# A gated image scan on one core: the bank of the neighbour sum, the grouping of the projections, the joined bypass and the issue order

## Chip, cores and metric

The kernel runs on one NeuronCore of a Trainium2 chip. The metric is the device time of one execution in microseconds (us). Everything is fp32. "PE" is TensorE, "DVE" VectorE, "ACT" ScalarE, "POOL" GpSimd.

## What is computed

Two layers run one after the other on x of shape (8, 192, 64, 64). Only the first is touched by the change. Cut to what matters, its scan is:

```python
x = conv3x3_depthwise(conv1x1(x, W_in)) + b_dw          # 384 channels
p = conv1x1(x, W_xd)                                    # 16 channels
Gl, Gm, Gr = normalize_w(W_w @ p)                       # each divided by |Gl|+|Gm|+|Gr|+1e-7
xs = stack of 4 directions of x                         # x, x^T, and both flipped
def step(h, (x, l, gl, gm, gr)):                        # 8 steps along chunks of 8
    return l * x + gl * h_up + gm * h + gr * h_down
out = scan(step) * (W_u @ p) + xs * (W_d @ p)
y = sum over directions d of w_m[d] * out[d]            # then layernorm, GRN, conv1x1
```

The second layer (layernorm and two Mamba passes over the tokens) takes the larger part of the time; its code is the same on both sides.

## The kernel before

**Stages.** For each of the 8 images, `project` makes the depthwise convolution `xc` (three tiles of 128 channels) and the 16 proxy channels `xp`, `scan` runs the gated scan, `norm` and `project_out` finish. Only `scan` and the parts of `Step` that it calls are touched.

**Steps.** A scan has 96 steps: 3 channel tiles x 8 chunk positions j x 4 directions d, in this order, d innermost. One step works on 128 channels x 512 pixels. Its state is `h{d}`, so that step (j, d) needs the state of the step four before it. A step with j = 0 has no previous state: it has no gates, no neighbours, no normalization, and its state is simply lam times x.

**Parts of a step.** The six projections are matmuls of 16 rows (L237), each on its own 32-row group of the array by `ROWS`: GL group 0, GM 1, GR 2, GLAM 3 (`gates`), GU group 0 and GD group 1 (`up`). Then:

- `magnitude` (ACT, L250 for the first two, L247 in place for the third) takes absolute values; `norm` (DVE, L278, two adds) sums them in the third gate's bank; `log` and `exp` (ACT, L283, L288) and `newton` (DVE, L294, L295) make the reciprocal.
- `neighbour` (DVE, L263, three products of a gate with the shifted state); `pair` (POOL, L267) adds two of them; `total` (PE, L273, two identity matmuls) sums the rest in PSUM; `mix` (DVE, L299) multiplies by the reciprocal.
- `decay` (ACT, L254) copies the lam projection out of PSUM, `entry` (POOL, L257) multiplies it by x, `state` (POOL, L303) makes the new state.
- `direct` (ACT, L310) copies the D projection out of PSUM, `bypass` (POOL, L313) multiplies it by x; `output` (DVE, L319, `hu`) multiplies the U projection by the state.
- `add` (PE, L329, identity matmuls) sums `hu` and `dx` of the four directions in bank `yp`; `store` (ACT, L339, after every fourth step) copies it out.

**The joined bypass.** With `JOINED = 2`, direction 2 does not send its `dx` to PE; at direction 3 an extra POOL add (L315) puts the two `dx` together, and one matmul takes both.

**PSUM.** There are eight banks: `gl`, `gm`, `q`, `yp` one each, `gr` and `c` two each. `c` turns over three tiles in each step: the lam projection, the D projection and the U projection. The sum over neighbours has `q`.

**The order.** The steps are software-pipelined. One iteration of `scan` issues parts of five steps, named `s3` (oldest) to `s0` and `ahead` (next). The order of the lines in that loop is the order in each engine's queue; every engine works its own queue in order and waits where an operand or a buffer is not ready. In the loop PE gets, in order: total, gates, add, add, up.

Of the kernel before, what the change touches and what calls it, by code (L numbers as in the profile page):

```python
# [22 lines left out]
ND = 4  # L23
# [7 lines left out]
SLOTS = NC * GROUPS  # L31
FAR = (0, 5, 6, 10, 21, 23)
ACT_SET = "natural_log_exp_and_others"
JOINED = 2
GL, GM, GR, GLAM, GU, GD = range(6)

ROWS = {GL: (0, 0), GM: (1, 0), GR: (2, 0), GLAM: (3, 0), GU: (0, 1), GD: (1, 1)}
# [3 lines left out]
def kernel(ctx: ExitStack, tc: tile.TileContext, x, w_in, dw, vecs, w_xd, w_gate, w_m, w_out, mid):  # L41
# [4 lines left out]
    nc = tc.nc  # L46
# [10 lines left out]
    def bank(tag, name, shape=(P, T)):  # L57

        return ps.tile(list(shape), F32, tag=tag, name=name, bufs=2 if tag in ("gr", "c") else 1)


    ident = const.tile([P, P], F32, name="ident0")
# [139 lines left out]
    def direction(xc, d, j):  # L202

        if d % 2 == 0:
            at = j if d == 0 else CHUNK - 1 - j
            v = xc.rearrange("p h (n j) -> p j n h", j=CHUNK)[:, at]
        else:
            at = j if d == 1 else CHUNK - 1 - j
            v = xc.rearrange("p (n j) w -> p j n w", j=CHUNK)[:, at]
        return v if d < 2 else v[:, ::-1, :]  # L210

    def flat(ap):
        return ap.rearrange("p n h -> p (n h)")
# [4 lines left out]
    class Step:  # L218
# [19 lines left out]
            return dst  # L238

        def gates(self):  # L240
            self.pl = self.gate(GLAM, "c")
            if self.j:
                self.g = [self.gate(kind, tag) for kind, tag in ((GL, "gl"), (GM, "gm"), (GR, "gr"))]

# [23 lines left out]

        def total(self):
            if self.j:  # L270
                self.sum = bank("q", f"q_{self.tag}")
                for i, term in enumerate((self.q[2], self.q[0])):
                    nc.tensor.matmul(self.sum, ident, flat(term), start=(i == 0), stop=(i == 1))  # L273

# [36 lines left out]

        def bypass(self):
            nc.gpsimd.tensor_mul(self.dx, self.dx, direction(self.xc, self.d, self.j))  # L313
            if self.d == JOINED + 1:
                nc.gpsimd.tensor_add(self.dx, self.dx, self.before.dx)  # L315

        def output(self):
            self.hu = self.work("hu")
# [1 line left out]

        def add(self, i):


            if self.d == 0 and i == 0:
                self.yp = bank("yp", f"yp_{self.tag}")
            elif i == 0:
                self.yp = self.before.yp
            if i == 0 or self.d != JOINED:
                nc.tensor.matmul(  # L329
                    self.yp,  # L330
                    ident,
                    flat((self.hu, self.dx)[i]),
                    start=(self.d == 0 and i == 0),
                    stop=(self.d == ND - 1 and i == 1),
                )

        def store(self):
            if self.d == ND - 1:
# [8 lines left out]
    def scan(b, xc, xp):  # L347


        ys, steps = [], [Nothing()] * 4  # L350
        for c in range(NC):
            wg = w_gate_sb[:, :, :, c * P : (c + 1) * P]
            ys.append(big.tile([P, CHUNK, CHUNK * HW], F32, tag="big", name=f"y_{b}_{c}"))
            for j in range(CHUNK):
                steps += [Step(f"{b}_{c}_{j}_{d}", xc[c], xp, wg, d, j) for d in range(ND)]
                for step in steps[-ND:]:
                    step.y = ys[c][:, j, :]
        for before, step in zip(steps[4:], steps[5:]):
            step.before = before
        steps += [Nothing()] * 4  # L360
        for s3, s2, s1, s0, ahead in zip(steps, steps[1:], steps[2:], steps[3:], steps[4:]):
            s2.state()
            s0.neighbour(2)
            s0.neighbour(0)
            s0.entry()
            s1.newton()
            s1.total()
            s0.neighbour(1)
            s0.pair()
            s0.magnitude(2)  # L370
            s2.direct()
            ahead.gates()
            s0.norm()
            s0.log()
            ahead.decay()
            s2.bypass()
            s3.add(0)
            s2.output()
            s3.add(1)
            ahead.magnitude(0)  # L380
            s1.up()
            s0.exp()
            s1.mix()
            ahead.magnitude(1)
            s3.store()
        return ys

    def norm(b, ys):
# [112 lines left out]
    with tc.manual_schedule():  # L501
        leaving = iter(())
        for b in range(B):
            xc, xp = project(b, leaving)
            ys = scan(b, xc, xp)
            leaving = project_out(b, ys, norm(b, ys))
        for _ in leaving:
            pass
# [497 lines left out]
```

## Time and profile before

| | us |
|---|---|
| median of 3 runs (17370.91 to 17383.58) | 17378.43 |
| the profiled execution, its own time | 17372.38 |
| its span, first to last instruction | 17370.6 |
| the 8 scans together (first lam copy to last y copy of each) | 4463.8 |
| each scan | 551.4 to 565.5 |
| first layer, about | 6080 |

A page of the profile lists busy time by engine, the span in 40 slices, the chain of work that ended last, and groups of instructions with mean duration. The timeline lists instructions of one engine in order: start, duration, line, tiles, count, and in brackets the idle time before it with what ended it. An fp32 matmul shows as two records; "x4" is two matmuls. "PEclk" is the granted share of TensorE's full clock. Durations overlap a little where an engine is fed without a break: DVE products last 0.68 us but start 0.60 us apart.

### The profile page before, as it was taken

Reading aid. Unit: us, or ns where it says so; the run is one execution under the profiler, and the core shown is the slowest. Engines: PE = TensorE matmul, PEld = TensorE weight load, DVE = VectorE, ACT = ScalarE, POOL = GpSimd, SP = SyncE. Lnnn points to the kernel's source line nnn. Section 1 sums busy time; section 2 is a strip of 40 time slices with the busy share of each in tenths; the row PEclk is TensorE's granted clock in tenths of the full one; section 3 lists DMA queues with packets and bytes.
Section 4 is the critical chain, followed back from the end, with each engine's and each line's share of the span. In section 5 each row is a group of like instructions: output and inputs, shape, how many; then the busy total and the mean of one; then the engine's idle time right before and its main releaser. Section 6 shows DMA issues by size and latency. Waiting matters only on the chain.

```text
span 17370.6 us, 150062 instructions
## 1 busy us (share of the span) xinstructions
PE 16036.3 (92%) x42192; PEld 6487.9 (37%) x42192; DVE 15678.3 (90%) x17290; ACT 11433.8 (66%) x21275; POOL 15638.3 (90%) x9538
## 2 busy tenths in 40 slices
PE   8999999999999889999999999999999999999998
PEld 2333333333333334333334434344434343434433
DVE  8888878878888689999999999999999999999999
ACT  5656666566666566666666666666666666666666
POOL 7787967869787699999999999999999999999999
PEclk8999999999999999999999999999999999999999
DMA  0000000000000022222222222222222222222222
GB/s 13 10 6 15 1 15 4 11 15 1 15 1 13 13 102 102 102 102 102 103 101 103 102 103 101 97 99 96 100 101 102 102 102 102 103 102 103 102 103 81
DMA packets 392024, 1195.85 MB, mean 69 GB/s; under 512 B 43736, under 2 KB 110640, under 8 KB 389648
## 3 DMA queue, kind: packets, MB, share of 16 engines
q1 hardware_dynamic: 390784, 1185.97, 19.7%
q8 instruction: 330, 5.41, 0.1%
q14 instruction: 510, 4.18, 0.1%
q10 hardware_dynamic: 400, 0.29, 0.0%
HBM read 1127.39 MB, written 58.72 MB: 68 GB/s over the span
## 4 chain that ended last, share of the span: by engine, by line
POOL 23%; DVE 17%; PE 11%; ACT 11%; issue 8%; DMA 1%; POOLq 0%; DVEq 0%; SPq 0%; ACTq 0%
DVE da L799 12%; POOL hs L786 12%; ACT da L792 4%; POOL hs L813 4%; PE yp L818 3%; DVE hs L813 2%; PE pc L670 2%; DVE hs L799 2%; POOL lg L725 2%; POOL dt L727 2%; POOL e L723 2%; PE pi L648 1%; PE g L237 1%; ACT xc L683 1%; POOL dtx L730 1%
## 5 line engine op out<-in xcount | busy, mean ns | idle before, releaser
L786 POOL TENSOR_TENSOR hs<-dtx,b_sb 128x1024 f32<-128x1024 f32 x3072 | 7163.0, 2359 | 91.5 <-PE yp L818 69.9
L818 PE MATMUL yp<-hs,ident 128*128 128x512 f32 x12288 | 5814.5, 616 | 509.2 <-DVE hs L813 303.9
L799 DVE TENSOR_TENSOR_SCAN da<-da,state,hs 128x512 f32<-128x512 f32 x4032 | 5183.2, 1286 | 227.0 <-ACT state L809 140.3
L792 ACT ACTIVATE da<-dt,a 128x512 f32<-128x512 f32 x6144 | 4245.2, 691 | 195.2 <-POOL dt L727 4.1
L818 PEld LDWEIGHTS yp<-hs,ident 128*128 128x128 f32 x12288 | 2325.7, 196 | 3668.1 <-issue 2487.7
L813 DVE TENSOR_TENSOR hs<-da,c_sb 128x1024 f32<-128x1024 f32 x2304 | 2815.3, 1222 | 139.5 <-DVE da L799 2.7
L237 PE MATMUL g<-xp,w_gate_sb 16*128 16x512 f32 x8640 | 1815.6, 658 | 60.4 <-ACT dx L310 51.6
L809 ACT COPY state<-da 128x2 f32<-128x2 f32 x2304 | 358.1, 155 | 2293.8 <-DVE hs L813 2290.3
L813 POOL TENSOR_TENSOR hs<-hs,c_sb 128x1024 f32<-128x1024 f32 x768 | 1810.0, 2357 | 12.4 <-ACT state L809 12.4
L648 PE MATMUL pi<-xT,in_w 96*128 96x512 f32 x3072 | 1513.0, 630 | 264.6 <-ACT xc L674 174.9
L799 DVE TENSOR_TENSOR_SCAN hs<-da,state,hs 128x512 f32<-128x512 f32 x1344 | 1624.3, 1263 | 106.4 <-ACT state L809 106.4
L670 PE MATMUL pc<-xr,conv_diag 128*128 128x512 f32 x3072 | 1489.0, 615 | 5.3 <-POOL xr L659 3.0
L263 DVE TENSOR_TENSOR q<-g,h 128x512 f32<-128x512 f32 x2016 | 1352.0, 684 | 116.1 <-PE g L237 71.4
L273 PE MATMUL q<-q,ident 128*128 128x512 f32 x2688 | 1336.3, 620 | 0.0
L313 POOL TENSOR_TENSOR dx<-dx,xc 128x512 f32<-128x512 f32 x768 | 1080.1, 1406 | 158.6 <-ACT dx L310 136.9
L283 ACT ACTIVATE rc<-g,eps 128x512 f32<-128x512 f32 x672 | 462.4, 688 | 1115.0 <-DVE g L278 1115.0
L267 POOL TENSOR_TENSOR q<-q,q 128x512 f32<-128x512 f32 x672 | 853.7, 1270 | 197.4 <-DVE q L263 193.0
L648 PEld LDWEIGHTS pi<-xT,in_w 96*128 96x128 f32 x3072 | 597.1, 199 | 1104.0 <-issue 649.8
L237 PEld LDWEIGHTS g<-xp,w_gate_sb 16*128 16x128 f32 x8640 | 495.6, 188 | 1307.0 <-DVE q L263 392.0
L257 POOL TENSOR_TENSOR lam<-lam,xc 128x512 f32<-128x512 f32 x672 | 942.8, 1403 | 33.5 <-ACT lam L254 33.5
L163 POOL TENSOR_TENSOR xc<-xc,side 128x504 f32<-128x504 f32 x384 | 450.6, 1174 | 559.5 <-DVE xc L158 297.3
L278 DVE TENSOR_TENSOR g<-g,ab 128x512 f32<-128x512 f32 x1344 | 933.1, 694 | 22.8
(135 smaller groups left out, 23252.6 us busy)
## 6 DMA issues: line engine op xcount, KB each, us to landing
b_sb<-bc SPq DMA_DIRECT2D x1024, 512.0 KB, 7.2
c_sb<-bc SPq DMA_DIRECT2D x1024, 512.0 KB, 6.3
xin<-in_x_dram SPq DMA_DIRECT2D x64, 384.0 KB, 3.6
mid<-ot SPq DMA_DIRECT2D x16, 1536.0 KB, 8.4
xt<-mid SPq DMA_DIRECT2D x64, 384.0 KB, 5.0
out_dram<-y SPq DMA_DIRECT2D x64, 384.0 KB, 2.6
bc<-dbl SPq DMA_DIRECT2D x128, 64.0 KB, 1.6
in_w<-in_in_w_dram SPq DMA_DIRECT2D x2, 576.0 KB, 5.8
```

Of the source, the lines that this page charges most:

```text
L237: nc.tensor.matmul(dst, self.wg[r, at, self.d, :], flat(self.xp[r, self.j]), start=True, stop=True)
L257: nc.gpsimd.tensor_mul(self.lam if self.j else self.hc, self.lam, direction(self.xc, self.d, self.j))
L263: nc.vector.tensor_mul(self.q[i], rows(self.g[i]), self.h[:, :, i : i + HW])
L273: nc.tensor.matmul(self.sum, ident, flat(term), start=(i == 0), stop=(i == 1))
L313: nc.gpsimd.tensor_mul(self.dx, self.dx, direction(self.xc, self.d, self.j))
L648: nc.tensor.matmul(pi, self.m.in_w[:, i, c * P : (c + 1) * P], self.tokens.xT[:, i, :], start=(i == 0), stop=(i == 1))
L670: nc.tensor.matmul(pc, self.m.conv_w[:, c, t, :], self.xr[c][:, t : t + T], start=(t == 0), stop=(t == 3))
L786: nc.gpsimd.tensor_mul(self.hs, dtx, self.p.b_sb[self.g])
L792: nc.scalar.activation(self.da[:, n, :], self.p.dt[self.c], AF.Exp, scale=self.p.m.a[:, self.c, at : at + 1])
L799: nc.vector.tensor_tensor_scan(self.h[:, n, :], self.da[:, n, :], self.hs[:, n, :], 0.0 if self.p.k == 0 else self.state[:, n : n + 1], AL ...
L813: engine.tensor_mul(self.hs, self.h, self.p.c_sb[self.g])
L818: nc.tensor.matmul(self.p.yp[self.c], ident, self.hs[:, n, :], start=False, stop=stop)
```

## The change

Four things at once, all in the first layer's scan:

1. The lam projection goes to bank `q` (it was in `c`), and the sum over neighbours goes to `gl`, the bank that held the first gate (it was in `q`). So `total` has to wait until the first gate was read, and the next first gate until `mix` has read the sum.
2. `up` and `gates` stand next to each other, so that PE gets six 16-row projections in a row, and the adds and the total (four 128-row matmuls) in a row.
3. The joined bypass is gone: every direction sends its own `dx` to PE, and POOL has no extra add.
4. The whole order of the loop is another. `entry` is one iteration later, the first two `magnitude` parts one iteration later.

```diff
-JOINED = 2
...
         def gates(self):
-            self.pl = self.gate(GLAM, "c")
+            self.pl = self.gate(GLAM, "q")
...
         def total(self):
             if self.j:
-                self.sum = bank("q", f"q_{self.tag}")
+                self.sum = bank("gl", f"q_{self.tag}")
...
         def bypass(self):
             nc.gpsimd.tensor_mul(self.dx, self.dx, direction(self.xc, self.d, self.j))
-            if self.d == JOINED + 1:
-                nc.gpsimd.tensor_add(self.dx, self.dx, self.before.dx)
...
-            if i == 0 or self.d != JOINED:
-                nc.tensor.matmul(
+            nc.tensor.matmul(
...
         for s3, s2, s1, s0, ahead in zip(steps, steps[1:], steps[2:], steps[3:], steps[4:]):
+            s3.add(0)
+            s0.neighbour(0)
+            s3.add(1)
+            s0.magnitude(0)
+            s0.neighbour(2)
+            s2.direct()
             s2.state()
-            s0.neighbour(2)
-            s0.neighbour(0)
-            s0.entry()
+            s0.neighbour(1)
+            s2.bypass()
+            s1.total()
+            s0.magnitude(2)
             s1.newton()
-            s1.total()
-            s0.neighbour(1)
+            s2.output()
+            s1.mix()
+            s0.magnitude(1)
+            s1.up()
+            ahead.gates()
             s0.pair()
-            s0.magnitude(2)
-            s2.direct()
-            ahead.gates()
+            s3.store()
+            s1.entry()
             s0.norm()
+            ahead.decay()
             s0.log()
-            ahead.decay()
-            s2.bypass()
-            s3.add(0)
-            s2.output()
-            s3.add(1)
-            ahead.magnitude(0)
-            s1.up()
             s0.exp()
-            s1.mix()
-            ahead.magnitude(1)
-            s3.store()
         return ys
```

More of the change, by code (lines that the diff above doesn't have):

```diff
@@ L327, in add @@
                 self.yp = self.before.yp
-            if i == 0 or self.d != JOINED:
[L329 to L335, printed above, removed]
+            nc.tensor.matmul(
+                self.yp,
+                ident,
+                flat((self.hu, self.dx)[i]),
+                start=(self.d == 0 and i == 0),
+                stop=(self.d == ND - 1 and i == 1),
+            )
         def store(self):
```

## Prediction, made before the changed kernel was run

> **What bounds it now.** I read the page's slices first (the scans lie in the first 14 of 40, the rest is the second layer, which keeps its code), then the busy time by stretch inside one scan, then PE's timeline of one step, then DVE's and ACT's.
>
> ```profile
> 204.00:227.00 23.00, 23.00 (x80) 7.48 (x78) 22.58 (x37) 15.44 (x30) 22.06 (x18) 1.00 0.00 0
> 227.00:250.00 23.00, 23.00 (x80) 7.49 (x78) 22.57 (x37) 15.45 (x30) 21.84 (x17) 1.00 0.01 1
> 319.00:346.00 27.00, 24.13 (x54) 7.11 (x56) 7.63 (x12) 7.83 (x14) 16.38 (x13) 0.75 0.00 0
> ```
>
> Columns: stretch, its length, busy PE, PE weight loads, DVE, ACT, POOL, granted clock, DMA. The first two rows are four steps with j > 0 (the y copies stand 22.97 apart there): PE never stops, DVE and POOL are within 5% of full. Three engines are nearly tied, so relief on PE alone is worth at most the distance to the next. The third row is the passage from one channel tile to the next, where four steps have j = 0: DVE is idle for most of it and TensorE has only 0.75 of its clock.
>
> ```profile
> 307.22 1.98 PE L273 MATMUL q<-q,ident 128*128 128x512 f32 x4
> 309.13 1.14 PE L237 MATMUL g<-xp,w_gate_sb 16*128 16x512 f32 x8
> 310.20 1.12 PE L329 MATMUL yp<-hu,ident 128*128 128x512 f32 x2
> 311.17 1.02 PE L329 MATMUL yp<-dx,ident 128*128 128x512 f32 x2
> 312.12 1.13 PE L237 MATMUL g<-xp,w_gate_sb 16*128 16x512 f32 x4
> ```
>
> One step of PE: total 1.91, four gates side by side 1.07, two adds 1.92, up 1.06; the next total follows at 313.18. That is 5.96. The step without its second add (direction 2) took 5.10. 3 x 5.96 + 5.10 = 22.98, the measured 22.97. A lone matmul costs 1.06 and a second one of the same form only 0.86 more, so every change between 128-row and 16-row form costs 0.20, four times per step.
>
> ```profile
> 308.90 1.42 DVE L278 TENSOR_TENSOR g<-g,ab 128x512 f32<-128x512 f32 x2
> 310.23 0.68 DVE L319 TENSOR_TENSOR hu<-g,h 128x512 f32<-128x512 f32 x1
> 310.83 0.68 DVE L299 TENSOR_TENSOR rc<-q,rc 128x512 f32<-128x512 f32 x1
> ...
> 310.36 0.69 ACT L283 ACTIVATE rc<-g,eps 128x512 f32<-128x512 f32 x1 [2.02 <-DVE g L278]
> 310.94 0.58 ACT L254 COPY lam<-g 128x512 f32<-128x512 f32 x1
> 311.41 0.61 ACT L250 ACTIVATE ab<-g 128x512 f32<-128x512 f32 x1
> 311.90 0.64 ACT L288 ACTIVATE rc<-rc 128x512 f32<-128x512 f32 x1
> 312.42 0.61 ACT L250 ACTIVATE ab<-g 128x512 f32<-128x512 f32 x1
> ```
>
> DVE's timeline stands above the dots, ACT's below. ACT waits 2.02 for the norm and then does other copies between log and exp; nothing of PE hangs on the end of this sequence today.
>
> **Engine sums after the change, j > 0.** PE: four 128-row matmuls 1.06 + 3 x 0.86 = 3.64; six projections in two rounds (GU and GL share group 0, GD and GM group 1) 1.06 + 0.86 = 1.92; together 5.56 in every step, against 5.74 on average now. The missing join costs PE 0.86 in one step of four, and that is in this sum. POOL loses the 1.27 us add (192 times, 244 us): from about 22 to about 21 in four steps; it is no longer near the limit. DVE keeps its nine operations: starts 0.60 apart, 0.72 where one reads the one before (newton, norm): 7 x 0.60 + 2 x 0.72 = 5.65. So by sums alone a step could fall from 5.74 to about 5.65.
>
> **The new waits, j > 0.** Sums don't set the step; two closed loops through the engines do.
>
> *Loop A* (the `gl` bank and ACT's order). `total` may not write `gl` before the first magnitude has read it; that magnitude now stands behind log and exp of the step before in ACT's queue; log waits for norm, norm stands behind mix on DVE, mix waits for total. Round it goes: magnitude 0.61, to PE 0.05 (matmuls start 0.05 after an ACT release elsewhere), total 1.98 to its last end, to DVE 0.04, mix to norm 0.60, norm 1.42, to ACT 0.04, log 0.69, exp 0.03 behind it, exp to magnitude 0.52 (311.90 to 312.42). Sum 5.98.
>
> *Loop B* (banks `c` and `gl`). First neighbour to hu on DVE 0.60 + 0.60 + 0.60 + 0.72 + 0.61 = 3.13, hu 0.68, to PE 0.05, GU 0.53 + 0.43, GL behind it in the same row group 0.43 + 0.59, to DVE 0.04. Sum 5.88.
>
> Loop A is longer than all sums: 5.98 per step, 23.9 for four, +0.93 against 22.97. Behind the waiting total stand up and gates, behind ACT's log stand exp and the first magnitude. Bounds: the first weight load of a group is exposed (1.06 against 0.86 includes about 0.1 of it); if it hides under the wait, A is 5.87 and B 5.78, that is +0.5 for four steps. If total's wait for two engines costs 0.1 more, as DVE's starts after two semaphores do here, 6.08, +1.35. I take 5.98, since every term is a row. A scan has 18 such intervals between y copies: 18 x 0.93 = +16.7 (+9 to +24).
>
> **The passages with j = 0.** Two in each scan. The two y intervals of a passage sum to 49.2 on average over all 16 (44.5 to 55.1). Here PE waits for ACT:
>
> ```profile
> 328.60 2.08 PE L237 MATMUL g<-xp,w_gate_sb 16*128 16x512 f32 x4
> 331.42 2.07 PE L237 MATMUL g<-xp,w_gate_sb 16*128 16x512 f32 x2 [0.74 <-ACT dx L310]
> 333.42 2.08 PE L329 MATMUL yp<-hu,ident 128*128 128x512 f32 x2
> 335.29 1.91 PE L329 MATMUL yp<-dx,ident 128*128 128x512 f32 x2
> ```
>
> lam, D and U turn over two `c` banks, so the next lam projection waits for the D copy of the step before; that spreads the matmuls, the clock is halved (2.08 where 1.13 stood), and this delays the copies again. After the change lam has its own bank, and between two passages of 16-row work lie only adds. PE's work for the eight steps: two normal 2 x 5.98, two with total but one row round 4.70, two with neither 2.97, two with six projections and no total 3.84: 34.9. Following the new order through with these durations leaves PE waiting about 2 us for hu (three times 0.3 to 0.9). I take 37.1 at full clock. Bounds: 34.9, and 44.6 if as much is lost beyond PE's work as today (the same count gives 39.5 of 49.2 now, 9.7 over). Gain per passage 12.1 (4.6 to 14.3), twice per scan: -24.2.
>
> **A rule against the row.** The Trainium skill, "TensorE: Matmul & The Clock Gate", Part 1, The HAM clock gate, says that the clock returns to half after at least one idle window of about 3.4 us. Between 319 and 346 the longest pause of PE is 0.74 us, and yet the clock is 0.75: a stretch thinly filled with 16-row matmuls is enough. By the rule the passage would hold no half clock to win back: PE ran at half for a half of 27 us, 6.7 us of it lost, so 42.5 and a gain of 5.4; the scan would come out at 16.7 - 10.8 - 0.7 = +5.2, or +42 us in all. By the row the gain is 12.1. I take the row.
>
> The ends of a scan (first lam copy, last flush of 14.3) change by under 1 us: -0.7, from GL's shorter way at the start and the later store. The stages around the scan keep their instructions; the second layer is as before.
>
> **Sum.** Per scan +16.7 - 24.2 - 0.7 = -8.2; eight scans -66. The profiled execution 17372 gives 17306; the median of the runs is 6 above that execution, so 17312.
>
> **Rivals.**
> 1. *The passages stay cold* (slower side). If the j = 0 stretch keeps today's losses, the gain is 4.6 each: 16.7 - 9.2 - 0.7 = +6.8 per scan, +54, 17432. It decides from a gain below 8 per passage. For it: the clock fell without a long pause. Against: the cause of the pauses, the shared `c` bank, goes. 17%.
> 2. *The loops are shorter* (weight loads hidden): +9 - 24.2 - 0.7 = -16 per scan, -127, 17251. For it: loads are hidden wherever the group is busy. 22%.
> 3. *Passages warm, but loop A at 6.08*: 24 - 24.2 - 0.7 = -1 per scan, 17371, no change. 14%.
> 4. *The six projections don't run as two rounds*, so that GL, GM and GR follow one by one: PE +0.86 or more per step, 6.4, above loop A; 18 x 2.6 = 47, +180 us. The four gates side by side in 1.07 speak against it. 3%.
> The forecast as it stands: 44%.
>
> Forecast and rival 2 lie below -0.2% (-35 us, what a measurement of this kernel can tell from no change), with a part of the first near it: faster 0.66, within 0.2% 0.18, slower 0.16. The range runs from rival 2 with the shorter passages (17230) to rival 1 (17430).
>
> **What would show it.** y copies 23.9 apart inside a channel tile (22.97 now); PE no longer at 100% there, with `total` waiting about 0.3 for ACT's magnitude; log, exp and magnitude in one unbroken row; passages of 37 with the clock at 1.00; no L315 on POOL. Wrong would be: passages above 41, y copies below 23.4 or above 24.4, or any change in the second layer beyond a few us.

## The result, and the profile after

The changed kernel takes 17363.65 us (median of 12 runs, 17340.23 to 17373.36) and the kernel before, run on the same chip, 17373.88 us (12 runs, 17366.26 to 17383.58). The ratio is 0.9992, with an interval of 0.9983 to 1.0000: no change by the bound of 0.2%. The forecast was 17312, a change of -66 us that did not come; its range, 17230 to 17430, held the time because it reached from well below to above the kernel before. The profiled execution took 17365.81 us, its span 17364.0 (before: 17370.6).

The intervals between y copies, taken from the trace, say where the scan's time went. "Passage" is the sum of the two y intervals of a j = 0 stretch, "head" the time from the first lam copy to the first y copy, "flush" the last y interval.

| per scan | forecast of the change | before | after | difference |
|---|---|---|---|---|
| 18 steady intervals | +16.7 | 22.98 | 24.19 | 18 x 1.21 = +21.7 |
| 2 passages | -24.2 | 49.15 (44.5 to 55.1) | 37.9 (37.3 to 39.0) | 2 x -11.25 = -22.5 |
| flush | -0.7 with the head | 14.29 | 17.69 | +3.4 |
| head | | 31.7 | 28.89 | -2.8 |
| sum | -8.2 | | | -0.2 |

So the gain in the passages is there, and the slower steps give it back. All eight scans together take 4462.4 us (4463.8 before): 1.4 less. The spans differ by 6.6 us, and 6.4 of that lie behind the last scan, in code that is the same on both sides, so nothing shows that the 10 us between the medians come from the scan. The head is no fixed time: in the changed kernel it takes 26.1 to 33.5 us, with 6.8 to 23.9 us of it at half clock by the trace's clock records, which list the stretches at each granted clock (31.6 to 31.8 and 13.7 before).

The busy time by stretch of the changed kernel (stretch, its length, PE, PE weight loads, DVE, ACT, POOL, granted clock, DMA): four steps with j > 0, then a passage.

```profile
204.00:228.00 24.00, 23.09 (x81) 7.94 (x80) 22.53 (x37) 15.77 (x29) 20.88 (x17) 1.00 0.00 1
318.00:344.00 26.00, 25.26 (x79) 8.66 (x80) 16.66 (x26) 14.12 (x26) 23.29 (x18) 1.00 0.01 1
```

In the first row no engine is full any more: PE 96%, DVE 94%, POOL 87%. A stretch that no engine fills and that still repeats exactly points to a chain of waits through several of them. In the second row the clock is 1.00 where it was 0.75. PE's timeline of one step of the changed kernel shows the wait:

```profile
254.08 1.98 PE L272 MATMUL q<-q,ident 128*128 128x512 f32 x4 [0.23 <-ACT ab L249]
255.99 1.99 PE L236 MATMUL g<-xp,w_gate_sb 16*128 16x512 f32 x12
257.91 1.13 PE L324 MATMUL yp<-hu,ident 128*128 128x512 f32 x2
258.87 1.02 PE L324 MATMUL yp<-dx,ident 128*128 128x512 f32 x2
260.12 1.98 PE L272 MATMUL q<-q,ident 128*128 128x512 f32 x4 [0.23 <-ACT ab L249]
```

The totals are 6.04 apart, and each waits 0.23 for a magnitude of ACT. ACT in the same step:

```profile
258.23 0.69 ACT L282 ACTIVATE rc<-g,eps 128x512 f32<-128x512 f32 x1 [0.36 <-DVE g L277]
258.95 0.63 ACT L287 ACTIVATE rc<-rc 128x512 f32<-128x512 f32 x1
259.49 0.58 ACT L249 ACTIVATE ab<-g 128x512 f32<-128x512 f32 x1
```

Log, exp and magnitude stand in one row, as loop A has it. DVE, where log's wait for the norm begins:

```profile
256.10 0.69 DVE L298 TENSOR_TENSOR rc<-q,rc 128x512 f32<-128x512 f32 x1 [0.23 <-PE q L272]
256.70 1.49 DVE L277 TENSOR_TENSOR g<-g,ab 128x512 f32<-128x512 f32 x2
258.11 1.88 DVE L262 TENSOR_TENSOR q<-g,h 128x512 f32<-128x512 f32 x3
259.90 0.69 DVE L293 SCALAR_TENSOR_TENSOR g<-g,rc 128x512 f32<-128x512 f32 x1
...
261.23 0.68 DVE L316 TENSOR_TENSOR hu<-g,h 128x512 f32<-128x512 f32 x1
```

Mix waits for total (0.23), the norm pair follows and log follows that. All links of loop A can be read off these three views.

### The profile page after: what moved, and what is told of

Same layout as the page of the kernel before. It is cut to its first block, busy times and chain, and to the rows that moved or that the text cites. A ratio compares the mean times of both kernels' runs of the same rounds, so it can differ in the third digit from the quotient of the medians.

```text
span 17364.0 us, 152244 instructions
## 1 busy us (share of the span) xinstructions
PE 15944.2 (92%) x42576; PEld 6558.0 (38%) x42576; DVE 15697.1 (90%) x17290; ACT 11507.9 (66%) x21275; POOL 15419.6 (89%) x9346
## 4 chain that ended last, share of the span: by engine, by line
POOL 22%; DVE 18%; ACT 11%; PE 9%; issue 8%; DMA 0%; POOLq 0%; DVEq 0%; SPq 0%; ACTq 0%
DVE da L794 12%; POOL hs L781 12%; ACT da L787 4%; POOL hs L808 4%; PE yp L813 3%; DVE hs L808 3%; PE pc L665 2%; DVE hs L794 2%; POOL lg L720 2%; POOL dt L722 2%; POOL e L718 1%; PE pi L643 1%; ACT xc L678 1%; POOL dtx L725 1%; ACT z L679 1%
## 5 line engine op out<-in xcount | busy, mean ns | idle before, releaser
L236 PE MATMUL g<-xp,w_gate_sb 16*128 16x512 f32 x8640 | 1544.4, 630 | 26.8 <-ACT lam L253 10.7
L262 DVE TENSOR_TENSOR q<-g,h 128x512 f32<-128x512 f32 x2016 | 1262.1, 681 | 98.6 <-PE g L236 96.2
L253 ACT COPY lam<-g 128x512 f32<-128x512 f32 x768 | 449.4, 585 | 1330.1 <-PE g L236 1269.2
L157 DVE SCALAR_TENSOR_TENSOR xc<-pi,dw_sb,xc 128x504 f32<-128x504 f32 (+3 forms) x1152 | 834.2, 736 | 105.2 <-ACT xc L135 58.5
L302 POOL TENSOR_TENSOR h<-lam,rc 128x512 f32<-128x512 f32 x672 | 859.0, 1278 | 54.5 <-DVE rc L298 1.9
```

What stands on the lines that cost most here:

```text
L236: nc.tensor.matmul(dst, self.wg[r, at, self.d, :], flat(self.xp[r, self.j]), start=True, stop=True)
L262: nc.vector.tensor_mul(self.q[i], rows(self.g[i]), self.h[:, :, i : i + HW])
```

## The experiments

The theory was loop A: total waits for the magnitude, which stands behind log and exp, which wait for norm, mix and the total before. The expectations call it A. Its rivals were the count of matmuls on PE, loop B (first neighbour, hu, adds and gates in the same row group), and, for the passages, the half clock against the order of work. Line numbers of an experiment can differ from those of the changed kernel by a few.

**1. The join put back into the changed kernel.**

```diff
+            if self.d == JOINED + 1:
+                nc.gpsimd.tensor_add(self.dx, self.dx, self.before.dx)
...
+            if i == 0 or self.d != JOINED:
                 nc.tensor.matmul(self.yp, ident, flat((self.hu, self.dx)[i]), ...)
```

> The changed kernel with the joined bypass restored: one add less on TensorE in every fourth step, one 1.27 us add more on GpSimd. Theory A (the closed loop total, mix, norm, log, exp, first magnitude, total sets the step; TensorE waits 0.23 us in it): the y copies stay 24.2 apart (24.1 to 24.4) and the time stays within 25 us of the changed kernel's 17364. Rival P (the number of matmuls sets the step, so that the dropped join is what made it slower): 0.86 less in four steps, 23.3, and about 124 us less in all, 17240.

Measured: 17433.4 us (5 runs, 17422.0 to 17444.9), ratio 1.0035 (1.0023 to 1.0047). In undisturbed stretches the y copies stay 24.18 apart although PE does one add less per four steps, so PE's count of matmuls does not set the step. But the time rose by 70 us, not within 25: the steady intervals average 24.34 because 13 of 144 are about 25.9, the passages are 40.77 and the flush 19.24. By the clock records each of these 13 holds one stretch of 3.41 us at half clock and no steady interval of the changed kernel holds any; all eight scans spend 268 us at half clock, 126 in the changed kernel. PE's timeline in a passage of this kernel, then at the same place of the changed kernel, shows how it comes about:

```profile
333.42 1.12 PE L328 MATMUL yp<-hu,ident 128*128 128x512 f32 x2
335.67 1.14 PE L237 MATMUL g<-xp,w_gate_sb 16*128 16x512 f32 x6 [1.13 <-DVE hu L319]
336.74 1.99 PE L328 MATMUL yp<-hu,ident 128*128 128x512 f32 x2
338.51 1.90 PE L328 MATMUL yp<-dx,ident 128*128 128x512 f32 x2
```

```profile
335.29 1.13 PE L324 MATMUL yp<-hu,ident 128*128 128x512 f32 x2
336.25 1.02 PE L324 MATMUL yp<-dx,ident 128*128 128x512 f32 x2
337.55 1.14 PE L236 MATMUL g<-xp,w_gate_sb 16*128 16x512 f32 x6 [0.28 <-DVE hu L316]
```

PE waits 1.13 for a hu where the changed kernel waits 0.28. The hu is not later: in front of it DVE waits 2.02 for POOL's state, 2.03 in the changed kernel. PE is earlier, by the add that direction 2 no longer sends. In the 3.42 us up to 336.86 PE is busy for 2.29 (in the changed kernel, from 335.30, for 3.13 of 3.41); then the granted clock is 0.50, and the adds take 1.99 and 1.90 where 1.13 and 1.02 stand at full clock. POOL's restored add, L315, comes behind that:

```profile
334.85 1.26 POOL L313 TENSOR_TENSOR dx<-dx,xc 128x512 f32<-128x512 f32 x1
336.19 1.27 POOL L315 TENSOR_TENSOR dx<-dx,dx 128x512 f32<-128x512 f32 x1
337.42 1.52 POOL L257 TENSOR_TENSOR h<-lam,xc 128x512 f32<-128x512 f32 x1
```

It stands ahead of the state product, and DVE waits 3.35 for that before the next hu (2.01 in the changed kernel). So removing the join is worth about 70 us to this order, and mainly because PE's extra add keeps the clock up: at the 0.44 us that a us at half clock costs in the passages (run 4), the 141 us make 62 of the 71 us by which the scans differ. That is an estimate; no run restored the one add without the other.

**2. The first magnitude moved ahead of exp, in the hope of cutting loop A.**

```diff
-            s0.magnitude(0)
...
             s0.log()
+            ahead.magnitude(0)
             s0.exp()
```

> The changed kernel with the first magnitude issued for the next step between log and exp, as the kernel before had it. Theory A: the loop loses the 0.54 us of exp and falls to 5.5, so the next loop (first neighbour, hu, U projection, GL behind it in row group 0) takes over at 5.88: y copies 23.5 apart, 18 x 0.66 x 8 = 95 us less than the changed kernel, about 17269. Rival P (matmuls set the step) and rival B (the loop through row group 0 sets it already): y copies stay at 24.2, time 17364.

Measured: 18093.4 us (18082.9 to 18103.3), ratio 1.0414 (1.0400 to 1.0429); y copies 28.65 apart. The expectation failed. What DVE does in two steps of this kernel:

```profile
251.20 1.89 DVE L262 TENSOR_TENSOR q<-g,h 128x512 f32<-128x512 f32 x3 [1.24 <-ACT ab L249]
...
258.27 1.89 DVE L262 TENSOR_TENSOR q<-g,h 128x512 f32<-128x512 f32 x3 [1.24 <-ACT ab L249]
```

The first neighbour and the first magnitude both read the bank of GL, and where two engines read one bank here, the one issued second waits for the first. In the changed kernel the neighbour is issued first; here it waits 1.24 for the magnitude, which stands behind log, and log waits for the norm that DVE has just made. That closes another loop: log to magnitude 0.58, the magnitude and its release 0.63, the first neighbour to the norm's end 5.83, to ACT 0.03, together 7.07 a step, or 28.3 for four, as in the shortest of the intervals (28.26). The edit cut one loop and closed a longer one, so it said nothing about loop A.

**3. The same, with GU moved to another row group (cutting loop B too).** Edit: that of 2, and in `ROWS` `GU: (0, 1)` becomes `GU: (2, 1)`.

> As the run before, and the U projection in row group 2 instead of 0, so that GL no longer stands behind it. Theory A with the second loop behind it: both are cut, and the nine DVE operations are left, 5.72 to 5.8 per step: y copies 22.9 to 23.2 apart, about 150 to 180 us less than the changed kernel, 17190 to 17215. If the second loop is no limit, nothing changes against the run before.

Measured: 18089.0 us, ratio 1.0411 (1.0397 to 1.0425), y copies 28.65 apart: the loop of run 2 again, and as little said of A and B.

**4. The kernel before, with one matmul that nothing uses in the place of each total that j = 0 leaves out.** The results stay the same; PE only gets more 128-row work in the passages.

```diff
             if self.j:
...
+            else:
+                rows8 = self.xc[:, 0:CHUNK, :].rearrange("p h w -> p (h w)")
+                nc.tensor.matmul(bank("q", f"fill_{self.tag}"), ident, rows8, start=True, stop=True)
```

> The kernel before, with one 128-row matmul without use added to each step with j = 0, into the bank of the sum that such a step leaves free. It tests what the half clock costs in the passages. Theory C (the passage is slow because TensorE is filled so thinly there that its clock falls): the clock in the passages goes back to 1.00 and the two y intervals of a passage sum to about 42 instead of 49.2, in spite of the added work; y copies elsewhere stay at 22.97. Rival W (the passage is waits through the shared banks, the clock only accompanies them): 49 to 52.

Measured: 17320.3 us (17314.0 to 17324.5), ratio 0.9969 (0.9957 to 0.9981). A passage of this kernel, in the busy times by stretch:

```profile
315.00:342.00 27.00, 27.00 (x72) 8.26 (x70) 12.00 (x20) 11.32 (x22) 21.93 (x17) 1.00 0.00 1
```

PE is full and the clock is 1.00. The passages take 42.57 instead of 49.15 although they hold more work, while the y copies stay at 22.98; 15 of the 16 hold no stretch at half clock. So the half clock costs at least 6.6 us per passage. The kernel before says how much more: its 16 passages spend 6.8 to 30.7 us at half clock by the clock records, and their lengths lie within 0.2 us of 41.5 plus 0.44 for each of these us. At 17.5 us on average that makes 7.7 us, and in the changed kernel, with 1.1 us, 0.5. By this estimate the half clock is about 7 of the 11.25 us that the change gains per passage.

The head is 7.7 longer (39.42), which the expectation did not have: there the same matmuls do not hold the clock, which is at half for 17.1 us in six scans and 37.5 in two (13.7 before). Per scan 2 x -6.57 + 7.7 = -5.4, times eight -44, and the scans' sum is 4419.9, which is 43.9 less than before. Adding useless work made the kernel faster.

**5. Loop A cut in another way: exp moved behind the first magnitude.** The neighbour still comes first on the bank, so the loop of run 2 doesn't arise.

```diff
             s0.magnitude(0)
+            s1.exp()
...
             s0.log()
-            s0.exp()
```

> The changed kernel with one line moved: exp of a step stands behind the next step's first magnitude, one iteration later, so that the first neighbour product still comes ahead of the magnitude that reads the same bank. Theory A: the loop loses the 0.54 us of exp without a new wait of DVE for ACT; the loop through row group 0 (5.88) or ACT's queue (5.95) is next: y copies 23.5 to 23.8 apart instead of 24.18, 18 x 8 x 0.4 to 0.65 = 55 to 95 us less, 17270 to 17310. Rival B (the row group's loop sets the step already) or P (number of matmuls): 24.2, time 17364.

Measured: 17349.3 us (14 runs, 17337.7 to 17362.0), ratio 0.9982 (0.9974 to 0.9990); y copies 24.12 apart. PE's timeline:

```profile
253.62 1.88 PE L272 MATMUL q<-q,ident 128*128 128x512 f32 x4
255.43 2.47 PE L236 MATMUL g<-xp,w_gate_sb 16*128 16x512 f32 x12
257.82 1.13 PE L324 MATMUL yp<-hu,ident 128*128 128x512 f32 x2
258.79 1.02 PE L324 MATMUL yp<-dx,ident 128*128 128x512 f32 x2
259.64 1.88 PE L272 MATMUL q<-q,ident 128*128 128x512 f32 x4
```

Total waits for nothing now, loop A is gone, and the step is still 6.02. Only the six projections have grown, from 1.99 to 2.47. That is loop B, on DVE:

```profile
251.90 1.89 DVE L262 TENSOR_TENSOR q<-g,h 128x512 f32<-128x512 f32 x3
253.78 0.70 DVE L293 SCALAR_TENSOR_TENSOR g<-g,rc 128x512 f32<-128x512 f32 x1
...
255.12 0.68 DVE L316 TENSOR_TENSOR hu<-g,h 128x512 f32<-128x512 f32 x1
...
257.93 1.89 DVE L262 TENSOR_TENSOR q<-g,h 128x512 f32<-128x512 f32 x3
```

First neighbour to hu 3.22, hu 0.68, from hu's end over the projections in the same row group to the next neighbour 2.13, together 6.03. The edit itself lengthened it: first neighbour to hu is 3.13 in the changed kernel (258.11 to 261.23), and of the 0.09 more here 0.07 stand before newton (L293), which has to wait for the later exp; that ends at 253.74.

**6. Loop B cut alone: the changed kernel with GU in another row group** (`GU: (2, 1)`).

> The changed kernel with only the U projection moved to row group 2. Theory A: the loop through log, exp and the first magnitude is untouched, y copies 24.1 to 24.2 apart, time within 20 us of 17364. Rival B (the U projection ahead of GL in row group 0 sets the step): y copies fall to 23.2 or below, about 140 us less.

Measured: 17356.6 us (14 runs, 17332.5 to 17361.3), ratio 0.9984 (0.9976 to 0.9992); y copies 24.18 apart, and total waits as ever. The passages are 36.7, all at full clock, and the head is 27.2, so what little it gains lies outside the steps. PE's timeline of this kernel:

```profile
252.06 1.98 PE L272 MATMUL q<-q,ident 128*128 128x512 f32 x4 [0.23 <-ACT ab L249]
...
258.11 1.98 PE L272 MATMUL q<-q,ident 128*128 128x512 f32 x4 [0.23 <-ACT ab L249]
```

**7. Both loops cut: the edits of 5 and 6 together.**

> As e5_exp_late, and the U projection in row group 2 instead of 0, so that GL does not stand behind it. Theory A with loop B behind it: the nine DVE operations are left with a wait of under 0.1 for exp, 5.75 to 5.85 per step: y copies 23.0 to 23.4 apart, about 140 to 170 us less than the changed kernel, 17195 to 17225; it would beat both kernels. If loop B is no limit, the same as e5_exp_late.

Measured: 17205.5 us (17204.6 to 17212.8), ratio 0.9900 (0.9885 to 0.9915); y copies 23.33 apart. DVE's timeline of this kernel over a little more than a step:

```profile
251.99 0.70 DVE L293 SCALAR_TENSOR_TENSOR g<-g,rc 128x512 f32<-128x512 f32 x1
252.73 0.69 DVE L294 SCALAR_TENSOR_TENSOR rc<-g,rc 128x512 f32<-128x512 f32 x1
253.34 0.68 DVE L316 TENSOR_TENSOR hu<-g,h 128x512 f32<-128x512 f32 x1
253.93 0.69 DVE L298 TENSOR_TENSOR rc<-q,rc 128x512 f32<-128x512 f32 x1
254.54 1.49 DVE L277 TENSOR_TENSOR g<-g,ab 128x512 f32<-128x512 f32 x2
255.94 1.87 DVE L262 TENSOR_TENSOR q<-g,h 128x512 f32<-128x512 f32 x3
257.80 0.70 DVE L293 SCALAR_TENSOR_TENSOR g<-g,rc 128x512 f32<-128x512 f32 x1
```

No row has a wait in brackets, and each op starts before the one above it has ended or within 0.04 of that. From L293 to the next L293 it is 5.81, nine operations in a row: DVE now sets the step, near the 5.65 of the prediction's engine sum (0.07 more in the norm pair and 0.07 where newton waits for exp). Of the 24.19 us of four steps the cut of A in run 5 gained 0.07, the cut of B alone nothing (24.19), both together 0.86. Two loops of nearly one length hide each other, and only the pair shows what they cost. Per scan against the kernel before: steady 18 x 0.35 = +6.3, passages 2 x -12.9 = -25.7, flush +3.1, head -4.5, together -20.8, eight times -166; the scans' sum fell by 166.8. This version beats both kernels.

**8. The kernel before, with lam in a bank of its own where j = 0.** Edit: `self.gate(GLAM, "c")` becomes `self.gate(GLAM, "c" if self.j else "q")`. It does that part of the change alone to which the prediction gave the passages' stalls.

> The kernel before with one part of the change alone: in the steps with j = 0 the lam projection goes to the sum's bank, which such a step leaves free; it stays in c elsewhere, and order, joined bypass and sum are as before. Theory C (in the passages the lam projection waits in c for the D copy of the step before, PE thins out and loses its clock): the two y intervals of a passage fall from 49.2 to about 40 to 42 and the clock there is 1.00; y copies elsewhere 22.97; 16 passages x 7 to 9 = 110 to 145 us less than before, about 17230 to 17265. Rival O (the new order shortened the passages, the bank doesn't matter): passages stay at 47 to 50, time within 25 us of 17374.

Measured: 17323.2 us (17303.1 to 17332.9), ratio 0.9970 (0.9959 to 0.9981); y copies 23.0 apart, passages 46.3 on average. PE's timeline in one passage:

```profile
333.61 1.14 PE L237 MATMUL g<-xp,w_gate_sb 16*128 16x512 f32 x8 [0.67 <-ACT dx L310]
...
338.45 1.14 PE L237 MATMUL g<-xp,w_gate_sb 16*128 16x512 f32 x8 [0.72 <-ACT dx L310]
339.52 1.80 PE L329 MATMUL yp<-hu,ident 128*128 128x512 f32 x2
341.12 1.91 PE L329 MATMUL yp<-dx,ident 128*128 128x512 f32 x2
```

The wait for the D copy that the prediction put on lam stays, on other projections, and behind it the adds run at half clock. All passages still hold a stretch at half clock: those with one of 3.41 us take 42.7, those with 13.7 to 20.5 us take 47.6 to 50.5. So the bank that lam shared was a part of the stall (2.9 us per passage), not all of it, and by the 0.44 of run 4 nearly all of these 2.9 are clock (11.3 us at half on average instead of 17.5).

## Why the prediction came out as it did

**The mechanism was right, its largest term too small.** Loop A sets the step of the changed kernel: total waits for the magnitude (0.3 foreseen, 0.23 measured), and log, exp and magnitude follow one another. Its cycle was put at 5.98 and is 6.05. In the trace: magnitude to total 0.64 (0.66 foreseen), total 1.98, to mix 0.04, mix to norm 0.60, norm 1.49 (1.42), to log 0.04, log to exp 0.72, exp to magnitude 0.54 (0.52). The term that failed is the norm pair, put at the 1.42 of the old order: in the new order its second add starts 0.79 after the first, not 0.72. In the records this add now checks two semaphores, that of the add before it and that of ACT, where it checked one; ACT's magnitude has ended 2.0 us before, so the 0.07 go with the second check and not with a wait for ACT (no run took it away). 0.07 per step is 0.28 per four steps, and with 18 intervals and eight scans 40 of the 66 us that were forecast. The bound 6.08 of rival 3, for which the prediction gave "total's wait for two engines", is nearly what was measured: the cost of a second semaphore was foreseen, but at total and not at the norm.

**Loop B was put 0.10 below A, and in the changed kernel it does lie about 0.1 below.** 5.88 was foreseen. With the changed kernel's own 3.13 from first neighbour to hu and run 5's 2.13 from hu's end to the next neighbour it is 5.94, an estimate, since B does not bind there; 6.03 is what it grew to when run 5 moved exp. So a cut of A that left newton alone could have gained up to about 0.4 per four steps; the one that was tried gained 0.07.

**The passages** were put at 37.1 and are 37.9: two in each of eight scans, 13 us. Eleven of the 16 keep the full clock and take 37.3 to 37.7, five hold 3.41 us at half clock and take 38.9 or 39.0. The weighing held: each gains 11.25, near the 12.1 that followed from the row and not the 5.4 that followed from the rule of the Trainium skill ("TensorE: Matmul & The Clock Gate", Part 1, The HAM clock gate). Run 4 keeps the clock up by filling PE, and the passage loses 6.6 us with nothing else in it taken away. By the estimate there about 7 us of the gain are clock and the other 4 waits and order. The cause named for the stall, the bank that lam shares, is only a part (run 8).

**The ends** were put at -0.7 and are +0.6 (flush +3.4, head -2.8), 10 us in all. The flush was held to change by under 1 us, and that step failed. PE's timeline at the end of a scan of the changed kernel shows what the new order leaves there:

```profile
700.48 1.12 PE L324 MATMUL yp<-hu,ident 128*128 128x512 f32 x2
701.44 1.02 PE L324 MATMUL yp<-dx,ident 128*128 128x512 f32 x2
702.73 1.12 PE L324 MATMUL yp<-hu,ident 128*128 128x512 f32 x2 [0.27 <-DVE hu L316]
```

The last steps have no gates of a step ahead to fill PE, and each stage waits for the one before. By the code the chain of stages per step is longer than in the old order; that this is where the 3.4 us go, and how they divide, was not tried.

Together 40 + 13 + 10 = 63 of the 66 us. The case that came true is rival 3, passages warm and no net gain per scan (-1 foreseen, -0.2 measured), given 14%. Its price was known, as "+1.35 for four steps" (measured +1.21), and 0.1 us on a step of 6 decided between -66 us and nothing. That the time lies inside the stated range is due to the width of the range, not to the forecast.

**The other signs:** six projections run as two rounds (1.92 as foreseen, so rival 4 falls), no L315 on POOL, POOL less loaded. The second layer moved by a few us only.

## What to carry to other kernels

When a new order closes a loop of waits through several engines, add the loop up term by term and treat 0.1 us per turn as unknown: if the gain elsewhere is as small as that times the number of turns, forecast no change. Look for the second-longest loop before repairing the longest one, since here the cuts, each made alone, gave 0.07 us and nothing of 24.19 in the step, and the two together 1% of the whole time. A cut can also lengthen the next loop, as in run 5. A matmul taken from PE can cost more than it saves where it leaves PE thin enough for the clock to fall (run 1), and a useless one can pay (run 4). Check also which reader of a shared bank is issued first: the same operations in the other order cost 4%.

## What the runs showed that was not expected

- The granted clock falls to half in stretches of 3.41 us or a multiple of it although the longest pause of PE in the passages of the kernel before is 0.75 us; one extra 128-row matmul per step keeps it at 1.00 in 15 of 16 passages, but not in the heads (run 4), and one add less in four steps lets it fall in steady stretches too (run 1). The Trainium skill, "TensorE: Matmul & The Clock Gate", Part 1, The HAM clock gate, gives an idle window of about 3.4 us for the return to half; the pauses here are shorter. Further on, the same part tells of a kernel in which frequent short pauses did it, without a threshold.
- Two engines that read one PSUM bank keep the order of issue in this program, to the price of 1.24 us per step in run 2.
- Of four gates issued in a row in the kernel before, the one whose row group was still busy began at 151.456 us by the records, and the two behind it in the program at 151.254 and 151.261 (which is which follows from the weight loads, which began in program order at 151.239 to 151.259). The same skill page, Part 3, The mechanism, holds that matmuls start and end in program order; in these records matmuls of other row groups overtake a waiting one, so PE does not always work its queue in order.
- A DVE operation starts 0.60 us after an independent one, 0.72 after one whose result it reads, and 0.79 in the norm pair of the changed kernel, where it has to check ACT's semaphore too. In a loop with ten links this is the size that decided.
